# Loads on SyncE's queue in a graph kernel: a window slice from a doubled transpose, the destinations in one DMA, slice addresses made once, row registers loaded 32 at a time

## Chip, cores and metric

One NeuronCore of one Trainium2 chip. The metric is the device time of one execution in microseconds (us), over three runs; smaller is better. Engines go by the profile's names: PE (matmul), PEld (its weight loads), DVE, ACT, POOL (GpSimd) and SP (SyncE). "SPq", "ACTq" and "POOLq" are the queues in which these issue DMAs, load registers and wait.

## The reference

Per edge, a message from its two nodes and its attributes; a sum over the edges that end in a node; a node update with a residual and a layer norm (no scale or shift).

```
x (12500, 64)   src, dst (400000,)   edge_attr (400000, 16)      dst is sorted
m_in     = concat([x[src], x[dst], edge_attr])                   # 400000 x 144
messages = silu(silu(m_in @ W1 + b1) @ W2 + b2)                  # 400000 x 64
agg      = segment_sum(messages, dst, 12500)
h        = x + silu(concat([x, agg]) @ W3 + b3)
out      = (h - mean(h)) / sqrt(var(h) + 1e-5)
```

## The kernel before

**Tiling.** 400000 edges are 3125 tiles of 128 edges. Eight tiles are an oct (1024 edges; 391 octs), three octs a chunk. As dst is sorted, the destinations of an oct lie in a window of S = 48 nodes that begins at `base[o]`, the destination of the oct's first edge; the values of `base` lie in `bi` (one partition, 391 integers). Two tiles share a matmul: the even tile on features 0 to 63, the odd one on 64 to 127.

**The first layer has three parts, summed in PSUM.**

- *Source part*, x[src] times the first 64 rows of W1. In the first 12 octs (RAW) POOL gathers rows of x. Meanwhile a table `pa` of that product for every node is made (L177 to L191), and later octs gather rows of `pa`, 128 rows in an indirect DMA (L382), with no matmul but a transposition (L462). Two of the eight tiles of about half of the octs (196, `pairs`) come another way: ACT copies 72 columns an oct and DVE 64 (L308, L306) out of the resident transposed x at addresses loaded into registers (L299), and a matmul (L465) makes their product. 23 further pairs of tiles (`rpairs`) are fetched by SP row by row: each oct, `rows` loads 16 addresses from `rindex` into registers (L329) and issues 16 DMAs of one 256-byte row of `pa` (L333); 16 octs fill one tile `rx` (256 rows), which the oct after next takes (L462).
- *Destination part*, x[dst] times the next 64 rows of W1, plus b1. SP loads the window's slice of transposed x, 64 features by 48 nodes, twice side by side into `xr` (L401; 3 buffers), whose 65th row is ones. `window_product` (L406) multiplies it with `w1bb` to 96 rows by 128 columns, `window_copy` (L411) multiplies by `mask`, which keeps rows 0 to 47 for the even tile and rows 48 to 95 for the odd one, into rows 0 to 95 of `xw`. `compare_dst` (L433) makes the one-hot matrix `oh`: rows 0 to 47 compare each window node with the even tile's destinations, rows 48 to 95 with the odd one's. The destinations `dr` are loaded for a chunk by two DMAs, 48 equal rows each (L421).
- *Attribute part*: rows 96 to 127 of `xw` are the last 16 rows of W1, those of `oh` the attributes (L422). One matmul of `xw` and `oh` (L466) gives destination and attribute part together.

After silu (L469), the second layer (L478, L480) and its silu (L484), a second one-hot matrix `eh` (L439) sums the messages by window node (L493), and DVE adds the window into `agg` (L498). Node groups of 512 are finished as soon as their edges are (L501 to L568), and what is left after the last oct.

**The order of the work.** The loop at L641 writes the order of PE, ACT, DVE and SP out by hand; each works through its list in order. In iteration o, SP issues: index loads for columns and rows (L360, L344); sometimes a slice of `src` (L123); at a chunk's beginning `dr` and the attributes of the chunk of oct o+3 (L421, L422); the slice `xr` of oct o+3 (L401), before which, every fourth time, four bases are loaded into registers (L390); the 16 rows (L329, L333); and loads and stores of nodes. PE takes in iteration o: the window product of oct o+1, the first layer of oct o, the node products, the sums of oct o-4, the second layer of oct o-2. POOL only gathers, three octs ahead in the order of the program (L669), into five buffers: it stops when the buffer that it needs has not been read by L462. In the built program each DMA of SP waits for the eighth DMA ahead of it on the same queue to have landed.

`window_load` as it is:

```
def window_load(o):
    if o % 4 == 0:
        bases(ENG.SP, o)
    xr = xrs[o % 3]
    frm = xt[:, ds(winreg.pop((ENG.SP, o)), S)]
    nc.sync.dma_start(xr[:D], frm[:, None, :].to_broadcast([D, 2, S]))
    winrow[o] = xr
```

Of the kernel before, what the change touches and what calls it, by code (L numbers as in the profile page):

```python
# [9 lines left out]
F32 = mybir.dt.float32  # L10
BF16 = mybir.dt.bfloat16
I32 = mybir.dt.int32
U8 = mybir.dt.uint8
AF = mybir.ActivationFunctionType
OP = mybir.AluOpType
# [3 lines left out]
ENG = mybir.EngineType  # L19

P = 128
# [3 lines left out]
S = 48  # L25
# [10 lines left out]
ROWS = 16  # L36
# [11 lines left out]
@with_exitstack  # L48
def kernel(
    ctx: ExitStack,  # L50
    tc: tile.TileContext,
    x: bass.AP,
    xt: bass.AP,
    src_c: bass.AP,
    src_row: bass.AP,
    dst_c: bass.AP,
    dst_row: bass.AP,
    attr_t: bass.AP,
    dst_2: bass.AP,
    attr_2: bass.AP,  # L60
    base: bass.AP,
    w1: bass.AP,
    b1: bass.AP,
    w2: bass.AP,
    b2: bass.AP,
    w3: bass.AP,
    b3: bass.AP,
    out: bass.AP,
    edges: int,
):  # L70

    nc = tc.nc
    N, D = x.shape

    const = ctx.enter_context(tc.tile_pool(name="const", bufs=1))
    dram = ctx.enter_context(tc.tile_pool(name="dram", bufs=1, space=DRAM))
    pa = dram.tile([N, D], F32, name="pa")
    badi = const.tile([1, 1], I32, name="badi")
    ident = const.tile([P, P], F32, name="ident")  # L90
    make_identity(nc, ident)

    with ExitStack() as inner:
        windows(inner, tc, ident, badi, pa, x, xt, src_c, src_row, dst_c, dst_row, attr_t, dst_2, attr_2, base, w1, b1, w2, b2, w3, b3, out, edges)

    flag = nc.values_load(badi[0:1, 0:1], min_val=0, max_val=2 * P,
                          skip_runtime_bounds_check_because="a count of partitions")
    with tc.If(flag > 0):
        general(tc, ident, x, xt, src_c, dst_c, dst_row, attr_t, w1, b1, w2, b2, w3, b3, out, edges)


def windows(ctx, tc, ident, badi, pa, x, xt, src_c, src_row, dst_c, dst_row, attr_t, dst_2, attr_2, base, w1, b1, w2, b2, w3, b3, out, edges):
    nc = tc.nc
    N, D = x.shape
    NP = xt.shape[1]
# [4 lines left out]
    E = 2 * S  # L110
    const = ctx.enter_context(tc.tile_pool(name="fconst", bufs=1))

    fast = ctx.enter_context(tc.tile_pool(name="fast", bufs=1))
# [12 lines left out]
    bi = fast.tile([1, NO], I32, name="bi")  # L126
# [69 lines left out]
    bf = fast.tile([1, NO], F32, name="bf")  # L196
# [2 lines left out]
    nc.gpsimd.iota(rowi, pattern=[[1, S]], base=0, channel_multiplier=0)  # L199
    coli = fast.tile([P, 1], I32, name="coli")  # L200
    nc.gpsimd.iota(coli, pattern=[[0, 1]], base=0, channel_multiplier=1)
    colf = fast.tile([P, 2], F32, name="colf")
    nc.vector.tensor_copy(colf[:, 0:1], coli)
    nc.vector.tensor_scalar(colf[:, 1:2], colf[:, 0:1], float(S), None, op0=OP.is_ge)

    mask = fast.tile([P, P], F32, name="mask")
    nc.vector.memset(mask[:, :D], 0.0)
    nc.vector.memset(mask[:, D:], 1.0)
    nc.vector.tensor_scalar(mask, mask, colf[:, 1:2], None, op0=OP.is_equal)
    nc.vector.tensor_scalar(colf[:, 1:2], colf[:, 1:2], -float(S), None, op0=OP.mult)  # L210
    nc.vector.tensor_tensor(colf[:, 0:1], colf[:, 0:1], colf[:, 1:2], op=OP.add)

    wb = fast.tile([P, NO], F32, name="wb")
    wps = ctx.enter_context(tc.tile_pool(name="wps", bufs=1, space=PSUM))
# [3 lines left out]
    pb = mis.tile([P, NO], F32, name="mm")  # L218
    nc.tensor.matmul(pb, ones, bf, start=True, stop=True)
    nc.vector.tensor_copy(wb, pb)  # L220
    nc.vector.tensor_scalar(wn, pb, colf[:, 0:1], None, op0=OP.add)

    rel = dc.bitcast(F32)
# [11 lines left out]
    w1bb = fast.tile([D + 1, 2, D], F32, name="w1bb")  # L235
# [1 line left out]
    nc.sync.dma_start(w1bb[D:, :, :], b1.rearrange("(o s k) -> o s k", o=1, s=1).to_broadcast([1, 2, D]))  # L237
    xrs = []
    for k in range(3):
        t = fast.tile([D + 1, 2, S], F32, name=f"xr{k}")  # L240
        nc.vector.memset(t[D:], 1.0)
        xrs.append(t)
    xw = []
    for k in range(3):
        t = fast.tile([P, P], F32, name=f"xw{k}")
# [10 lines left out]
    with tc.tile_pool(name="gat", bufs=AHEAD + 2) as gat, tc.tile_pool(name="drp", bufs=2) as drp, \  # L256
# [15 lines left out]
        while True:  # L272
            o = RAW + -(-2 * P * (len(pairs) + 1) // RATE) + 2
# [39 lines left out]
        while True:  # L313
            o = RAW + -(-2 * P * (len(rpairs) + 1) // ROWS) + 1
            if o >= len(octs) - 1:
                break
            rpairs.append(o)
        single, rindex = {}, {}
        pab = pa[:, :].bitcast(U8).rearrange("n d -> (n d)")

        def rows(o):
            lo = (o - RAW) * ROWS
            j, e0 = lo // (2 * P), lo % (2 * P)
            if o < RAW or j >= len(rpairs):
                return
            if e0 == 0:
                single[rpairs[j]] = rx.tile([P, 2, D], F32, name="rx")
            t = single[rpairs[j]].bitcast(U8)
            _, regs = nc.values_load_multi_w_load_instructions(  # L329
                rindex[j][0:1, e0:e0 + ROWS], engines=(ENG.SP,), min_val=0, max_val=4 * D * (N - 1),  # L330
                skip_runtime_bounds_check_because="src names a node")
            for e, r in zip(range(e0, e0 + ROWS), regs):
                nc.sync.dma_start(t[e % P:e % P + 1, e // P, :], pab[ds(r, 4 * D)].rearrange("(o n) -> o n", o=1))  # L333

        def rbegun(o):
# [32 lines left out]
                    nc.vector.tensor_scalar(t[:, h], t[:, h], 4.0, float(XBASE[s] + XADDR), op0=OP.mult, op1=OP.add)  # L368

        winrow, winreg = {}, {}  # L370
        sums = psa.tile([P, 4, S], F32, name="pg")

        def gather(o):
# [13 lines left out]
        def bases(eng, o):  # L387

            n = min(4, NO - o)
            _, regs = nc.values_load_multi_w_load_instructions(  # L390
                bi[0:1, o:o + n], engines=(eng,), min_val=0, max_val=N - 1,
                skip_runtime_bounds_check_because="dst names a node")
            for i in range(n):
                winreg[eng, o + i] = regs[i]

        def window_load(o):
            if o % 4 == 0:
                bases(ENG.SP, o)
            xr = xrs[o % 3]
            frm = xt[:, ds(winreg.pop((ENG.SP, o)), S)]  # L400
            nc.sync.dma_start(xr[:D], frm[:, None, :].to_broadcast([D, 2, S]))  # L401
            winrow[o] = xr

        def window_product(o):
            pw = mis.tile([P, P], F32, name="mm")
            nc.tensor.matmul(pw[:E, :], winrow[o].rearrange("k s w -> k (s w)"), w1bb.rearrange("k s m -> k (s m)"),  # L406
                             start=True, stop=True)
            winrow[o] = pw

# [3 lines left out]
        def load(c, o0=0, o1=CT // OT):  # L413

            if c not in loaded:
                loaded[c] = (drp.tile([E, CT // 2 * P], I32, name="dr"), hot.tile([P, CT // 2 * P], F32, name="oh"))
            dr, oh = loaded[c]
            e = slice(o0 * OT // 2 * P, o1 * OT // 2 * P)
            d = slice(c * CT // 2 * P + e.start, c * CT // 2 * P + e.stop)
            for k in range(2):  # L420
                nc.sync.dma_start(dr[k * S:(k + 1) * S, e], dst_2[k:k + 1, d].to_broadcast([S, e.stop - e.start]))  # L421
            nc.sync.dma_start(oh[E:, e], attr_2[:, d])  # L422

        hots = {}
# [159 lines left out]
        for q in range(early):  # L584
            if q >= rest:
                break
            o = lead[due[q]] + LAST - 1
# [4 lines left out]
        for q0, q1 in batches:  # L592
            o = lead[due[q1 - 1]] + LAST - 1
# [28 lines left out]
        for o in range(min(AHEAD, NO)):  # L622
            gather(o)
        window_load(0)
        window_product(0)
        window_copy(0)
        load(0, 0, 1)
        load(0, 1, 3)
        window_load(1)
        window_load(2)  # L630
        relative(0, CT)
        lims = nv.tile([P, 2, LP], F32, name="lims")
# [5 lines left out]
        with tc.manual_schedule(engines={ENG.PE, ENG.Activation, ENG.DVE, ENG.SP}):  # L638
            compare_dst(0)
            compare_nodes(0)  # L640
            for o in range(NO + THIRD):  # L641
# [3 lines left out]
                for k in parts[3 * o - 3:3 * o] if o else []:  # L645
                    n = min(XC, NP - k)
# [23 lines left out]
                if o + 3 < NO and octs[o + 3][3]:  # L670
                    load(octs[o + 3][0])
                if o + 3 < NO:
                    window_load(o + 3)
                if o + 1 < NO:
                    window_product(o + 1)
                if o % 4 == 0 and 4 <= o < NO + 4:
                    bases(ENG.DVE, o - 4)
# [21 lines left out]
                if 30 <= o < 30 + 2 * LP and o % 2 == 0:  # L699
                    k = (o - 30) // 2  # L700
# [10 lines left out]
                address(o + 2)  # L711
                raddress(o + 2)
                rows(o)
                if o < NO:
                    for f, a in todo.get(o, []):
# [284 lines left out]
```

## Time and profile before

| | |
|---|---|
| three runs, median (lowest to highest) | 3422.63 us (3420.27 to 3425.53) |
| the profiled execution, time | 3420.95 us |
| its span in the trace | 3418.8 us |
| granted TensorE clock, mean | 0.697 |
| busy, ACT / POOL / DVE / PE / PEld | 91% / 74% / 71% / 67% / 45% |
| SP row DMAs (L333) | 5888 |
| indirect gathers (L382) | 2591 of `pa`, 96 of x |

The profile is one execution, recorded by the hardware. Its page sums up each engine, each group of instructions by line and the chain of work that ended last; the trace can be asked for waits, for single lines, and for all that ran in a stretch of time. Times of rows count from the span's start. A row of a group reads: line, engine, operation, output<-input, shapes, xcount | busy us, mean ns | idle time before it and what ended that. A row of waits reads: engine, line <- what it waited for: us in total, times, longest us. A row of a line of code reads: durations as minimum/median/maximum in ns. "issue" is time in which the engine waited for nothing that the profile shows.

### The profile page before, as it was taken

How to read it: one execution, taken by the hardware profiler on the slowest of the kernel's cores; microseconds unless marked ns; L12 is line 12 of the kernel's file. 1: busy time of each engine (PE TensorE's matmuls, PEld its weight loads, DVE VectorE, ACT ScalarE, POOL GpSimd, SP SyncE). 2: the span in 40 equal slices, each digit the busy share in tenths (PEclk: the TensorE clock that was granted, in tenths of full speed). 3: DMA queues.
4: the chain of work that ended last, by engine and by line, in shares of the span. 5: the costliest groups of instructions: out<-in, count | busy, mean ns of one | idle time of the engine just before them, and what ended most of it. 6: DMA issues, size and time to landing. Idle time of an engine off the chain costs nothing. (4 is left out here: it accounts for less than half of the span.)

```text
span 3418.8 us, 107012 instructions
## 1 busy us (share of the span) xinstructions
PE 2283.9 (67%) x13764; PEld 1545.4 (45%) x13764; DVE 2433.6 (71%) x26003; ACT 3109.1 (91%) x27413; POOL 2542.7 (74%) x2696
## 2 busy tenths in 40 slices
PE   6777776666666666666666656666667576666667
PEld 4545444444444444444444444434444354444444
DVE  2577777677776777778777777777787776877772
ACT  2499999999999999999999999998999999999992
POOL 7777777777777777777777777776777777777774
PEclk7756566676666777677676667776766766777766
DMA  6532233233333322323332233233223223332322
GB/s 136 119 64 61 62 65 65 62 63 67 69 61 65 66 61 63 68 60 66 72 62 59 62 69 60 62 69 66 62 61 68 61 61 69 65 62 60 69 60 58
DMA packets 202928, 229.05 MB, mean 67 GB/s; under 512 B 133023, under 2 KB 141413, under 8 KB 201301
## 3 DMA queue, kind: packets, MB, share of 16 engines
q1 hardware_dynamic: 101560, 122.63, 16.1%
q0 software_dynamic: 85984, 88.22, 13.8%
q10 hardware_dynamic: 14652, 11.26, 1.5%
q14 instruction: 615, 5.03, 0.5%
q8 instruction: 117, 1.92, 0.2%
HBM read 215.45 MB, written 6.40 MB: 65 GB/s over the span
## 5 line engine op out<-in xcount | busy, mean ns | idle before, releaser
L382 POOL DMA_INDIRECT ga<-pa,sc x2591 | 2449.8, 945 | 813.4 <-issue 702.5
L308 ACT COPY cx<-xs 64x4 uint8 x26568 | 2646.4, 187 | 60.7 <-issue 37.2
L306 DVE TENSOR_REDUCE cx<-xs 64x4 uint8 x23608 | 1684.2, 153 | 527.3 <-issue 477.2
L406 PE MATMUL mm<-w1bb,xr 65*96 65x128 f32 x782 | 234.6, 395 | 839.2 <-DMA xr<-in_xt 673.6
L466 PE MATMUL p<-oh,xw 128*128 128x512 f32 (+1 forms) x758 | 601.7, 890 | 0.0
L480 PE MATMUL p<-w2d,h 128*128 128x128 f32 x3126 | 571.7, 339 | 0.0
L406 PEld LDWEIGHTS mm<-w1bb,xr 65*96 65x96 f32 x782 | 141.0, 226 | 890.3 <-DMA xr<-in_xt 785.1
L493 PEld LDWEIGHTS pg<-eh,m 128*64 128x64 f32 x6250 | 283.0, 175 | 574.6 <-issue 368.2
L480 PEld LDWEIGHTS p<-w2d,h 128*128 128x128 f32 x3126 | 483.1, 236 | 114.7 <-issue 114.7
L493 PE MATMUL pg<-eh,m 128*64 128x48 f32 x6250 | 334.8, 263 | 104.8 <-DVE agg L498 101.8
L433 DVE TENSOR_TENSOR oh<-dr,wrow 96x512 f32<-96x512 int32 x391 | 263.6, 674 | 150.4 <-DMA dr<-in_dst 70.8
L462 PE MATMUL p<-ident,ga 128*128 128x128 f32 x1296 | 318.9, 372 | 68.4 <-DMA ga<-pa,sc 68.1
L469 ACT ACTIVATE h<-p 128x512 f32<-128x512 f32 x391 | 231.7, 592 | 144.8 <-PE p L466 99.9
L462 PEld LDWEIGHTS p<-ident,ga 128*128 128x128 f32 x1296 | 236.1, 196 | 84.6 <-issue 80.3
L484 ACT ACTIVATE m<-p 128x512 f32<-128x512 f32 x391 | 231.4, 592 | 43.5 <-PE p L480 31.2
L439 DVE TENSOR_TENSOR eh<-wrow,dc 128x384 f32<-128x384 f32 x391 | 214.3, 548 | 2.7
L498 DVE TENSOR_TENSOR agg<-agg,pg 128x48 f32 x391 | 78.2, 200 | 188.3 <-PE mm L533 113.3
L466 PEld LDWEIGHTS p<-oh,xw 128*128 128x128 f32 x758 | 179.6, 291 | 0.0
L478 PE MATMUL p<-b2r,one 3*128 3x512 bf16 x391 | 177.5, 454 | 0.0
L411 DVE TENSOR_TENSOR xw<-mm,mask 96x128 f32<-96x128 f32 x391 | 109.6, 280 | 23.1 <-PE mm L406 15.2
L382 POOL DMA_INDIRECT ga<-in_x,sc x96 | 90.8, 946 | 30.2 <-issue 28.0
L465 PE MATMUL p<-cx,w1d 128*128 128x128 f32 x392 | 109.9, 377 | 0.0
(84 smaller groups left out, 780.2 us busy)
## 6 DMA issues: line engine op xcount, KB each, us to landing
rx<-pa SPq DMA_DIRECT2D x5888, 0.2 KB
dr<-in_dst SPq DMA_DIRECT2D x260, 288.0 KB
ga<-pa,sc POOLq DMA_INDIRECT x2591
oh<-in_attr SPq DMA_DIRECT2D x130, 192.0 KB
xr<-in_xt SPq DMA_DIRECT2D x391, 24.0 KB
xs<-in_xt ACTq DMA_DIRECT2D x12, 512.0 KB
cxi<-in_src_row SPq DMA_DIRECT2D x196, 1.0 KB
pa<-v ACTq DMA_DIRECT2D x12, 256.0 KB
```

The lines of the kernel that those rows point to most:

```text
L306: nc.vector.tensor_reduce(to, frm[:, :, None], AX.X, OP.max)
L308: nc.scalar.copy(to, frm)
L382: nc.gpsimd.indirect_dma_start(out=ga[:, i, :], out_offset=None, in_=x if o < RAW else pa[:, :], in_offset=bass.IndirectOffsetOnAxis(ap=sc ...
L406: nc.tensor.matmul(pw[:E, :], winrow[o].rearrange("k s w -> k (s w)"), w1bb.rearrange("k s m -> k (s m)"), start=True, stop=True)
L433: nc.vector.tensor_tensor(oh[:E, :], dr[:, e:e + w], wn[:E, o:o + 1].to_broadcast([E, w]), op=OP.is_equal)
L439: nc.vector.tensor_tensor(eh[:, :n], row[:, None, :].to_broadcast([P, n, S]), rel[:, t0:t0 + n, None].to_broadcast([P, n, S]), op=OP.is_equal)
L462: nc.tensor.matmul(p1[:, i, :], g2.rearrange("p s d -> p (s d)"), ident, is_transpose=True, start=(i == c), stop=False, skip_group_check=True)
L466: nc.tensor.matmul(p1[:, :k], xw[o % 3], oh, start=False, stop=True, skip_group_check=True)
L469: nc.scalar.activation(h[:, :k], p1[:, :k], AF.Silu)
L480: nc.tensor.matmul(p2[:, 2 * i:2 * i + 2, :].rearrange("p s d -> p (s d)"), h[:, i, :], w2d, start=False, stop=(i == k - 1), skip_group_ch ...
L484: nc.scalar.activation(m[:, :n2], p2[:, :n2], AF.Silu)
L493: nc.tensor.matmul(pg[s * D:(s + 1) * D, :], m[:, i, :], eh[:, i, :], start=(i < 2), stop=(i >= n - 2), skip_group_check=True)
```

## The change

Four edits. (1) The host passes a second transposed x, `xt2`, in which each column stands twice in a row (node n in columns 2n and 2n+1), and the slice is one DMA of 64 rows of 2 x 48 neighbouring elements, addressed in bytes. Rows of the window product, of `xw` and of `oh` are thereby ordered node by node, even and odd tile in turn, and the mask and the window node of each row are made from the row number by a shift and an `and`. (2) So the destinations are one DMA of 96 rows, whose source alternates between the two rows of `dst_2`. (3) The bases are multiplied by 8 once by DVE, into the storage of `bf` (free once its matmul has read it), and SP loads the slice's byte address. (4) Row addresses are loaded 32 at a time, in even octs, and used in two octs. The number and order of the other DMAs and of the work of PE, ACT, DVE and POOL in the loop stay.

```diff
+    half = fast.tile([P, 2], I32, name="half")
+    nc.vector.tensor_scalar(half[:, 0:1], coli, 1, None, op0=OP.arith_shift_right)
+    nc.vector.tensor_scalar(half[:, 1:2], coli, 1, None, op0=OP.bitwise_and)
     colf = fast.tile([P, 2], F32, name="colf")
-    nc.vector.tensor_copy(colf[:, 0:1], coli)
-    nc.vector.tensor_scalar(colf[:, 1:2], colf[:, 0:1], float(S), None, op0=OP.is_ge)
+    nc.vector.tensor_copy(colf, half)
...
-    nc.vector.tensor_scalar(colf[:, 1:2], colf[:, 1:2], -float(S), None, op0=OP.mult)
-    nc.vector.tensor_tensor(colf[:, 0:1], colf[:, 0:1], colf[:, 1:2], op=OP.add)
...
+    bi8 = bf.bitcast(I32)
+    nc.vector.tensor_scalar(bi8, bi, 8.0, None, op0=OP.mult)
...
-        t = fast.tile([D + 1, 2, S], F32, name=f"xr{k}")
+        t = fast.tile([D + 1, 2 * S], F32, name=f"xr{k}")
...
-            _, regs = nc.values_load_multi_w_load_instructions(
-                rindex[j][0:1, e0:e0 + ROWS], engines=(ENG.SP,), min_val=0, max_val=4 * D * (N - 1),
-                skip_runtime_bounds_check_because="src names a node")
-            for e, r in zip(range(e0, e0 + ROWS), regs):
+            if o % 2 == 0:
+                _, rowreg[:] = nc.values_load_multi_w_load_instructions(
+                    rindex[j][0:1, e0:e0 + 2 * ROWS], engines=(ENG.SP,), min_val=0, max_val=4 * D * (N - 1),
+                    skip_runtime_bounds_check_because="src names a node")
+            for e in range(e0, e0 + ROWS):
+                r = rowreg.pop(0)
                 nc.sync.dma_start(t[e % P:e % P + 1, e // P, :], pab[ds(r, 4 * D)].rearrange("(o n) -> o n", o=1))
...
+        xt2b = xt2.bitcast(U8)
...
+            at, unit = (bi8, 8) if eng == ENG.SP else (bi, 1)
             _, regs = nc.values_load_multi_w_load_instructions(
-                bi[0:1, o:o + n], engines=(eng,), min_val=0, max_val=N - 1,
+                at[0:1, o:o + n], engines=(eng,), min_val=0, max_val=unit * (N - 1),
...
-            frm = xt[:, ds(winreg.pop((ENG.SP, o)), S)]
-            nc.sync.dma_start(xr[:D], frm[:, None, :].to_broadcast([D, 2, S]))
+            nc.sync.dma_start(xr[:D, :].bitcast(U8), xt2b[:, ds(winreg.pop((ENG.SP, o)), 8 * S)])
...
-            for k in range(2):
-                nc.sync.dma_start(dr[k * S:(k + 1) * S, e], dst_2[k:k + 1, d].to_broadcast([S, e.stop - e.start]))
+            nc.sync.dma_start(dr[:, e], dst_2[None, :, d].to_broadcast([S, 2, e.stop - e.start]))
             nc.sync.dma_start(oh[E:, e], attr_2[:, d])
...
+        "xt2": np.repeat(np.concatenate([x, np.zeros((P, d), x.dtype)]).T, 2, axis=1),
```

More of the change, by code (lines that the diff above doesn't have):

```diff
@@ L53 @@
     xt: bass.AP,
+    xt2: bass.AP,
     src_c: bass.AP,
@@ L93 @@
     with ExitStack() as inner:
-        windows(inner, tc, ident, badi, pa, x, xt, src_c, src_row, dst_c, dst_row, attr_t, dst_2, attr_2, base, w1, b1, w2, b2, w3, b3, out, edges)
+        windows(inner, tc, ident, badi, pa, x, xt, xt2, src_c, src_row, dst_c, dst_row, attr_t, dst_2, attr_2, base, w1, b1, w2, b2, w3, b3, out, edges)
     flag = nc.values_load(badi[0:1, 0:1], min_val=0, max_val=2 * P,
@@ L99, with windows @@
         general(tc, ident, x, xt, src_c, dst_c, dst_row, attr_t, w1, b1, w2, b2, w3, b3, out, edges)
-def windows(ctx, tc, ident, badi, pa, x, xt, src_c, src_row, dst_c, dst_row, attr_t, dst_2, attr_2, base, w1, b1, w2, b2, w3, b3, out, edges):
+def windows(ctx, tc, ident, badi, pa, x, xt, xt2, src_c, src_row, dst_c, dst_row, attr_t, dst_2, attr_2, base, w1, b1, w2, b2, w3, b3, out, edges):
     nc = tc.nc
@@ L317, in windows @@
             rpairs.append(o)
-        single, rindex = {}, {}
+        single, rindex, rowreg = {}, {}, []
         pab = pa[:, :].bitcast(U8).rearrange("n d -> (n d)")
@@ L405, in window_product @@
             pw = mis.tile([P, P], F32, name="mm")
-            nc.tensor.matmul(pw[:E, :], winrow[o].rearrange("k s w -> k (s w)"), w1bb.rearrange("k s m -> k (s m)"),
+            nc.tensor.matmul(pw[:E, :], winrow[o], w1bb.rearrange("k s m -> k (s m)"),
                              start=True, stop=True)
```

## The prediction

> **What bounds the kernel now.** I read the page first, then the waits, then POOL in stretches of 100 us, then the trace around single octs.
>
> ```profile
> span 3418.8 us, 107012 instructions
> PE 2283.9 (67%) x13764; PEld 1545.4 (45%) x13764; DVE 2433.6 (71%) x26003; ACT 3109.1 (91%) x27413; POOL 2542.7 (74%) x2696
> L382 POOL DMA_INDIRECT ga<-pa,sc x2591 | 2449.8, 945 | 813.4 <-issue 702.5
> ```
>
> By busy time ACT is the engine to look at. But 702.5 us of POOL's idle time is "issue": nothing that the profile shows held it. The waits say how it is made up:
>
> ```profile
> POOL ga L382 <- issue: 730.5, 2396, 0.3
> POOL ga L382 <- DMA ga<-pa,sc: 58.0, 190, 0.3
> POOL ga L382 <- PE p L462: 34.9, 38, 3.8
> PEld mm L406 <- DMA xr<-in_xt: 785.1, 209, 9.2
> ```
>
> The longest "issue" is 0.3 us: a pause of 0.3 us follows every gather, so a gather costs 1.25 us and not the 0.945 shown. Only the third row holds real stops (up to 3.8 us): the buffer was not free, because PE was late. And PE's great wait is for the slice `xr`.
>
> ```profile
> 2.76 1.11 POOL L382 DMA_INDIRECT ga<-in_x,sc  x1 [1.27 <-DMA sc<-in_src_c]
> 289.64 0.94 POOL L382 DMA_INDIRECT ga<-pa,sc  x1 [0.30 <-issue]
> 1994.96 0.95 POOL L382 DMA_INDIRECT ga<-pa,sc  x1 [0.30 <-issue]
> 3369.39 1.23 POOL L602 IOTA xs<- 128x393 int32 x1
> 3385.79 1.06 POOL L382 DMA_INDIRECT ga<-pa,sc  x1 [0.30 <-issue]
> 300.00:400.00 100.00, 75.60 (x81) 0.59 0.31 66
> 1800.00:1900.00 100.00, 75.61 (x81) 0.66 0.30 63
> 2300.00:2400.00 100.00, 70.40 (x76) 0.68 0.31 64
> 3000.00:3100.00 100.00, 72.23 (x76) 0.70 0.31 64
> ```
>
> These are gathers number 1, 230 and 1594, POOL's one other operation in the loop, gather 2687, then POOL's busy time in four stretches of 100 us (behind it granted clock, DMA share, GB/s). From 1 to 1594: 1992.2 / 1593 = 1.2506 us each, and the stretches up to 1900 us are full (75.6). At that pace the last would start at 2.76 + 2686 x 1.2506 = 3361.9 us, 3363 with L602 (1.23). It starts at 3385.8: **POOL is the bound, and loses some 23 us in stops, all in the second half**. Behind the last gather come 33 us of tail.
>
> Why there? Gathers 230 and 1594 end octs 30 and 230 (an oct is 6.87 gathers on average, by the code). The slices of the same octs on SP's queue:
>
> ```profile
> 278.77 0.63 SPq L401 DMA_DIRECT2D xr<-in_xt  x1
> 2008.64 0.60 SPq L401 DMA_DIRECT2D xr<-in_xt  x1
> SPq L333 <- DMA oh<-in_attr: 19.1, 47, 1.3
> SPq L401 <- PE p L466: 10.9, 24, 0.7
> SPq L333 <- DMA dr<-in_dst: 6.7, 12, 1.1
> SPq L333 <- DMA xr<-in_xt: 5.3, 14, 1.1
> ```
>
> SP's period is 1729.9 / 200 = 8.65 us an oct, POOL's 1705.3 / 200 = 8.53. SP falls behind by 0.123 us an oct: from 10.9 us ahead of the last gather of its oct to 13.7 us behind it. The four waits are the longest of SP's queue between 300 and 2000 us: 42 us of 1700. SP is not held, it is full. When its lag has eaten POOL's five buffers (the stretches are full to 1900 us), POOL stops too. One such place:
>
> ```profile
> 1016.42 5.11 SPq L333 DMA_DIRECT2D rx<-pa  x16
> 2330.72 0.79 SPq L421 DMA_DIRECT2D dr<-in_dst  x2
> 2331.61 0.69 SPq L422 DMA_DIRECT2D oh<-in_attr  x1
> 2332.48 0.61 SPq L401 DMA_DIRECT2D xr<-in_xt  x1
> 2334.66 5.44 SPq L333 DMA_DIRECT2D rx<-pa  x16
> 2336.21 0.68 DVE L433 TENSOR_TENSOR oh<-dr,wrow 96x512 f32<-96x512 int32 x1 [2.59 <-DMA dr<-in_dst]
> 2337.35 0.74 PE L406 MATMUL mm<-w1bb,xr 65*96 65x128 f32 x2 [5.99 <-DMA xr<-in_xt]
> 2339.21 0.94 POOL L382 DMA_INDIRECT ga<-pa,sc  x1 [3.81 <-PE p L462]
> ```
>
> (The first row is an oct without a wait: 5.11 / 16 = 0.32 us a row DMA.) The slice goes out at 2332.48, PE has it at 2337.35 after waiting 6 us, then L462 frees the buffer, and POOL goes on 3.5 us late.
>
> **The change part by part.** Nothing changes in the loop on POOL, PE, ACT or DVE: every term is SP's time per oct. To keep POOL from stopping, the drift over the 360 octs behind oct 30 must stay under the 24.6 us that the buffers took before: under 0.068 an oct, so SP must save 0.055.
>
> ```profile
> L329 SPq TENSOR_LOAD <-rxi x368: 972/1415/1439, 129.1 to 3327.2; - x184
> L390 SPq TENSOR_LOAD <-bi x98: 302/557/914, 7.7 to 3349.8; - x98
> L401 SPq ALU_OP  x391: 32/41/54, 8.3 to 3358.9; - x196
> L401 SPq DMA_DIRECT2D xr<-in_xt x391: 598/615/1432, 8.5 to 3359.0; - x196
> L421 SPq DMA_DIRECT2D dr<-in_dst x264: 311/408/1577, 9.3 to 3356.3; - x132
> L147 ACTq DMA_DIRECT2D xs<-in_xt x14: 472/558/702, 2.5 to 116.1; - x14
> L515 SPq DMA_DIRECT2D xa<-in_x x25: 331/366/579, 267.9 to 3360.3; - x25
> 5.04 0.57 DVE L220 COPY wb<-mm 128x391 f32<-128x391 f32 x1 [1.01 <-PE mm L219]
> ```
>
> *Register loads.* No load of 32 is in the trace. 4 registers take 302 ns at least, 16 take 972: 56 ns a register. The median of 16 is 1415; I read the 440 ns between as a start cost that is spared in the one oct of four where a base load stands just ahead. A pair of loads is 2 x (0.75 x 1415 + 0.25 x 972) = 2.61 us; one of 32 is 972 + 16 x 56 + 440 = 2.31. Saved 0.30 a pair, 0.15 an oct. Bounds: with the steepest slope of these rows, (1415 - 302) / 12 = 93 ns, it would take 2.90 (0.14 lost an oct); without the 440, 1.87 (0.37 saved). The Trainium skill, "DMA: Bandwidth & Descriptors", section "Latency and other measured facts", gives a register load a floor of about 600 ns; by that each load dropped is worth 0.3 us an oct instead of 0.15. The 302 ns of the row speak for the smaller value.
>
> *Slice address*: 41 ns of ALU an oct, saved. *Slice DMA*: 128 pieces of 192 bytes become 64 of 384. Rows for 64 pieces exist on ACT's queue (558 median, 472 least, 702 most), for 128 on SP's (366). I take 0.50: 0.115 saved; bounds 0.09 lost, 0.25 saved. *Destinations*: two of 408 (0.79 together) become one of 96 rows; nothing shows it. Between one of the old (408) and the two together; I take the old slice's 0.6: 0.2 a chunk, 0.07 an oct; bounds 0 and 0.13.
>
> *What it costs.* SP's DMAs wait for the eighth ahead. Behind `dr`, attributes and slice, the sixth row is the eighth behind `dr`. Before, the register load (1.4) stood between slice and rows; these waits were 19.1 + 6.7 + 5.3 = 31.1 us in 66 chunks, 0.47 each. Chunks begin in turn in even and odd octs. In an odd one no load stands there now: the sixth row is ready 0.6 + 0.4 + 0.5 + 0.3 (gaps) + 5 x 0.32 = 3.4 us behind `dr`, which lands up to 5.5 us behind its issue (2336.21 - 2330.72): a wait of 2.1, with base loads before half of them 1.9. In an even one the load of 2.3 covers it. On average 1.0 a chunk, 0.5 more than now: 0.18 an oct lost. Bounds: all waits go (0.16 saved), or every chunk waits 2.1 (0.54 lost).
>
> Sum: 0.15 + 0.04 + 0.115 + 0.07 - 0.18 = **0.2 us an oct saved; SP's period 8.45**, below POOL's 8.53. With SP no longer behind, PE gets slices early, and POOL runs at 1.25 us to the end. What is late next is POOL itself, on which nothing is changed.
>
> *Start.* The first base load now waits for DVE's multiplication, which stands behind L220 (ends 5.61, so ready about 6.2); SP comes to that load at 7.7. It costs nothing, and a few us there would be covered by POOL's buffers. The operations on row numbers are two fewer or three more of 0.15 us.
>
> *Time.* The profiled execution took 3420.95, 2.15 more than its span; the median of three is 1.7 higher, and stops that vary from run to run are part of that. 3418.8 - 23 + 2.15 = **3398 us**.
>
> **The rivals.** *Part of it*: SP saves between 0 and 0.055; the drift shrinks, POOL stops later and less: 3403 to 3416. For it: four of five terms are not in the trace. Chance 0.12.
>
> *Another engine holds the pace* (no difference). The Trainium skill, "Perfetto Trace Analysis", section "Identifying the Most-Contended Engine", takes the engine with the highest occupancy as the one to relieve; that is ACT, and SP's work would not matter. In rows:
>
> ```profile
> 300.00:2000.00 1700.00, 1129.01 (x6792) 763.52 (x6792) 1266.79 (x13759) 1628.77 (x14565) 1284.76 (x1361) 0.69 0.31 64
> PE mm L406 <- DMA xr<-in_xt: 673.6, 186, 13.9
> ```
>
> The first row has the busy times of PE, PEld, DVE, ACT and POOL in that order. ACT: 1628.8 us in 199 octs, 8.2 an oct, 0.3 below POOL's pace. For it: that is thin, and compute was never seen without SP's delay. Against it: PE waits for slices, not for ACT. If some other chain holds compute at 8.65, or SP's terms cancel: 3416 to 3428. Chance 0.10.
>
> *Slower: the single `dr` lands later than its halves did*, and SP, which works in order, waits for it. SP's other terms save 0.375 an oct, 1.1 a chunk; it turns when the waits of a chunk pass 0.47 + 1.1 = 1.6 us on average (I expect 1.0). Landing 2 us later, odd chunks would wait 3.9 and even ones 1.8: (2.85 - 0.47) / 3 - 0.375 = 0.42 an oct more, all of it POOL's: 360 x 0.42 = 150 us, about 3570. For it: the landing of one DMA of that size is not in the trace. Against it: the same bytes, issued over the same 0.8 us. Chance 0.12.
>
> **How the numbers follow.** Forecast 0.66 (3391 to 3403), part 0.12, none 0.10, slower 0.12. The likeliest is 3398. From 3391 (a shorter tail) to 3418 (all but the upper part of no change) lie about 8 in 10; the worst ends of all terms together (0.7 an oct lost, some 260 us) lie with the slower 0.12. 0.2% is 6.8 us, about what can be told from no change. Faster by more: 0.66 + 0.12 less a little, 0.77. Within: 0.11. Slower: 0.12.
>
> **What would show it.** Right: POOL 75.6 busy in every stretch of 100 us to 3300; waits of POOL for L462 under 15 us; the wait of L406 for `xr` far smaller; SP's L401 ahead of its oct's last gather, and waits of SP for PE in its place; one load of 32 at about 2.3 us, the slice at 0.5, `dr` at 0.6; rows waiting 2 us for `dr` in odd chunks. Wrong: L401 still drifting; long waits of L333 for `dr`; or ACT or DVE waits ahead of PE.

## The result, and the profile after

| | median (lowest to highest) | runs |
|---|---|---|
| before, beside it | 3424.08 us (3420.27 to 3430.72) | 4 |
| after | 3396.59 us (3396.16 to 3401.12) | 4 |

The ratio is 0.9921, 95% interval 0.9903 to 0.9939: faster by 0.6 to 1.0%. The forecast was 3398, its own range 3391 to 3403. The profiled execution of after took 3396.16 us, 1.8 more than its span.

The experiments below ran on several chips, and the kernel before takes 3412 to 3434 us on two of them and 5509 to 5539 on four, so each experiment is set only against runs of before on its own chip.

First the page of after: span, busy times, the gathers, and the packets of all DMAs.

```profile
span 3394.4 us, 106238 instructions
PE 2398.6 (71%) x13764; PEld 1581.2 (47%) x13764; DVE 2430.3 (72%) x26003; ACT 3108.1 (92%) x27413; POOL 2542.1 (75%) x2696
L388 POOL DMA_INDIRECT ga<-pa,sc x2591 | 2449.2, 945 | 790.0 <-issue 707.6
DMA packets 175783, 228.98 MB, mean 67 GB/s; under 512 B 105886, under 2 KB 114276, under 8 KB 174164
```

By these sums hardly anything happened: ACT, DVE and POOL are as busy as before to within 4 us, and PE is busier by 115 us at a slightly lower granted clock (0.684 against 0.697), without effect on the end. The gain shows in POOL's waits and in its stretches of 100 us (length, POOL's busy time, granted clock, DMA share, GB/s).

```profile
POOL ga L388 <- issue: 734.7, 2410, 0.3
POOL ga L388 <- DMA ga<-pa,sc: 54.9, 180, 0.3
POOL ga L388 <- PE p L467: 8.5, 28, 0.3
PEld mm L412 <- DMA xr<-in_xt: 433.9, 166, 7.8
```
```profile
300.00:400.00 100.00, 75.61 (x81) 0.59 0.30 66
1800.00:1900.00 100.00, 75.61 (x81) 0.62 0.30 64
2300.00:2400.00 100.00, 75.60 (x81) 0.74 0.29 65
3000.00:3100.00 100.00, 75.47 (x81) 0.70 0.28 63
```

L467 is the transposition that frees a gather's buffer. Its row fell from 34.9 us with stops of up to 3.8 to 8.5 us with nothing above 0.3, and 0.3 is the ordinary pause behind every gather: POOL never stops for a buffer now. The two late stretches hold 81 and 81 gathers, where before held 76 and 76. PE's wait for the slice is about half of what it was.

The timeline shows the two queues against each other: gathers 230, 1594 and 2687 on POOL, and the slices of octs 30 and 230 on SP.

```profile
278.53 0.52 SPq L407 DMA_DIRECT2D xr<-in_xt  x1
290.66 0.94 POOL L388 DMA_INDIRECT ga<-pa,sc  x1 [0.30 <-issue]
1983.46 0.47 SPq L407 DMA_DIRECT2D xr<-in_xt  x1
1995.56 0.94 POOL L388 DMA_INDIRECT ga<-pa,sc  x1 [0.30 <-issue]
3362.45 1.05 POOL L388 DMA_INDIRECT ga<-pa,sc  x1 [0.30 <-issue]
```

The slice goes out 12.1 us ahead of its oct's last gather at oct 30 and 12.1 ahead at oct 230; before, it went from 10.9 ahead to 13.7 behind. SP's period is (1983.46 - 278.53) / 200 = 8.525 us an oct, and POOL's (1995.56 - 290.66) / 200 is 8.525 too: SP no longer falls behind. The last gather starts at 3362.45 instead of 3385.79, 23.3 us earlier, and the tail behind it is 31.95 instead of 33.0: together the 24.4 us by which the span is shorter.

SP's instructions by line (least, median, most in ns); the last row is that of before, for the row above it:

```profile
L333 SPq TENSOR_LOAD <-rxi x184: 2287/2308/2336, 132.8 to 3271.9; - x184
L407 SPq DMA_DIRECT2D xr<-in_xt x391: 468/495/1306, 8.7 to 3330.4; - x196
L426 SPq DMA_DIRECT2D dr<-in_dst x132: 578/634/1502, 9.2 to 3316.0; - x132
L397 SPq TENSOR_LOAD <-bf x98: 307/556/837, 7.7 to 3301.9; - x98
L427 SPq DMA_DIRECT2D oh<-in_attr x132: 316/542/1596, 9.9 to 3329.9; - x132
L422 SPq DMA_DIRECT2D oh<-in_attr x132: 310/367/811, 10.5 to 3358.5; - x132
```

and SP's longest waits between 300 and 2000 us (us in total, times, longest):

```profile
SPq L338 <- DMA dr<-in_dst: 35.6, 33, 2.7
SPq L365 <- ACTq L302: 21.1, 19, 4.4
SPq L338 <- DMA oh<-in_attr: 18.0, 36, 1.1
...
SPq L338 <- DMA xr<-in_xt: 5.1, 12, 0.9
```

The row DMAs (L338) wait 58.7 us in 66 chunks, where they waited 31.1. A new wait stands beside them: L365 loads an index tile that ACT still reads. Over all rows of this view SP's waits for other engines come to 68 us, where they came to 37 before: SP is held by the others more than it was, and at these octs it is still 12 us ahead, no more and no less. The attributes' DMA, which nothing in the change touches, takes 0.17 us longer behind the new destinations.

### The profile page after: what moved, and what is told of

Its sections match the earlier page's. It is cut to its first block, busy times and chain, and to the rows that moved or that the text cites. A ratio compares the mean times of both kernels' runs of the same rounds, so it can differ in the third digit from the quotient of the medians.

```text
span 3394.4 us, 106238 instructions
## 1 busy us (share of the span) xinstructions
PE 2398.6 (71%) x13764; PEld 1581.2 (47%) x13764; DVE 2430.3 (72%) x26003; ACT 3108.1 (92%) x27413; POOL 2542.1 (75%) x2696
## 2 busy tenths in 40 slices
DMA packets 175783, 228.98 MB, mean 67 GB/s; under 512 B 105886, under 2 KB 114276, under 8 KB 174164
## 5 line engine op out<-in xcount | busy, mean ns | idle before, releaser
L471 PE MATMUL p<-oh,xw 128*128 128x512 f32 (+1 forms) x758 | 623.0, 919 | 0.0
L485 PE MATMUL p<-w2d,h 128*128 128x128 f32 x3126 | 604.5, 353 | 0.0
L498 PEld LDWEIGHTS pg<-eh,m 128*64 128x64 f32 x6250 | 301.0, 184 | 619.9 <-issue 381.9
L485 PEld LDWEIGHTS p<-w2d,h 128*128 128x128 f32 x3126 | 512.0, 248 | 124.2 <-issue 124.2
L467 PE MATMUL p<-ident,ga 128*128 128x128 f32 x1296 | 358.8, 374 | 296.6 <-DMA ga<-pa,sc 295.5
L412 PE MATMUL mm<-w1bb,xr 65*96 65x128 f32 x782 | 226.1, 383 | 471.1 <-DMA xr<-in_xt 357.7
L498 PE MATMUL pg<-eh,m 128*64 128x48 f32 x6250 | 354.1, 273 | 131.7 <-DVE agg L503 118.7
L467 PEld LDWEIGHTS p<-ident,ga 128*128 128x128 f32 x1296 | 232.5, 190 | 366.3 <-issue 340.7
L483 PE MATMUL p<-b2r,one 3*128 3x512 bf16 x391 | 187.3, 479 | 0.0
```

Source lines behind the costliest of these rows:

```text
L412: nc.tensor.matmul(pw[:E, :], winrow[o], w1bb.rearrange("k s m -> k (s m)"), start=True, stop=True)
L467: nc.tensor.matmul(p1[:, i, :], g2.rearrange("p s d -> p (s d)"), ident, is_transpose=True, start=(i == c), stop=False, skip_group_check=True)
L471: nc.tensor.matmul(p1[:, :k], xw[o % 3], oh, start=False, stop=True, skip_group_check=True)
L485: nc.tensor.matmul(p2[:, 2 * i:2 * i + 2, :].rearrange("p s d -> p (s d)"), h[:, i, :], w2d, start=False, stop=(i == k - 1), skip_group_ch ...
L498: nc.tensor.matmul(pg[s * D:(s + 1) * D, :], m[:, i, :], eh[:, i, :], start=(i < 2), stop=(i >= n - 2), skip_group_check=True)
```

## The experiments

The theory was that of the prediction: SP's queue, full, delays the slices, PE frees POOL's buffers late, and the change takes 0.2 us an oct from SP, of which only what POOL lost can come back. Rival A: the fewer packets (202928 to 175783) or shorter transfers bring the gain, not the time of SP's queue. Rival B: only all edits together are enough, or one edit that was not priced as decisive carries it.

### The slice alone

Before, with edits 1 and 3 (slice of 64 rows, addresses made once). The register loads stay as before; the node-by-node order of rows needs every second partition in the two DMAs of `dr`:

```diff
-                nc.sync.dma_start(dr[k * S:(k + 1) * S, e], dst_2[k:k + 1, d].to_broadcast([S, e.stop - e.start]))
+                nc.sync.dma_start(dr[k:E:2, e], dst_2[k:k + 1, d].to_broadcast([S, e.stop - e.start]))
```

> The same kernel as in e2_slice_alone, beside runs of the kernel before on the same chip, since those of e2_slice_alone stood at 5528 us for the kernel before. Where the kernel before takes 3420 to 3431 us again: theory (SP's queue time): 615 - 495 ns of the DMA and 41 ns of ALU saved, 0.16 us an oct, no new wait: SP's period 8.49, under POOL's 8.53; POOL never stops, 3397 us (3394 to 3402). Rival 'the loads are the whole gain': 3422. Rival 'fewer packets': 3397.

Measured: 3396.6 us (3394.98 to 3402.23, 5 runs) against 3420.59 (8 runs), ratio 0.9935, interval 0.9914 to 0.9956. That can't be told from the whole change. SP's lines, then the two queues in the timeline:

```profile
L405 SPq DMA_DIRECT2D xr<-in_xt x391: 468/515/907, 8.4 to 3329.6; - x196
L425 SPq DMA_DIRECT2D dr<-in_dst x264: 511/577/1332, 9.0 to 3317.3; - x132
```
```profile
279.29 0.52 SPq L405 DMA_DIRECT2D xr<-in_xt  x1
289.88 0.94 POOL L386 DMA_INDIRECT ga<-pa,sc  x1 [0.30 <-issue]
1992.51 0.51 SPq L405 DMA_DIRECT2D xr<-in_xt  x1
1994.20 0.94 POOL L386 DMA_INDIRECT ga<-pa,sc  x1 [0.30 <-issue]
3361.76 0.97 POOL L386 DMA_INDIRECT ga<-pa,sc  x1 [0.30 <-issue]
```

SP's period is 1713.22 / 200 = 8.566 us an oct, POOL's 1704.32 / 200 = 8.522. Between these octs SP still falls behind, by 0.044 an oct (10.6 us ahead at oct 30, 1.7 at oct 230), but that is under the 0.068 that the prediction worked out as bearable. Behind oct 230 it falls back no farther: the slice of oct 380 goes out at 3270.79, 8.522 us an oct. PE still waits 685.7 us for slices:

```profile
PEld mm L410 <- DMA xr<-in_xt: 685.7, 186, 8.8
POOL ga L386 <- PE p L466: 10.4, 34, 0.3
```

and POOL doesn't stop once over 0.3 us. So the time is decided by whether the drift eats POOL's five buffers before the end, not by how long PE waits. The period was 0.08 longer than expected (8.49). Each of the two `dr` DMAs takes 577 ns instead of 408 when it writes every second partition, 0.34 a chunk or 0.11 an oct, and the attributes' DMA behind them 536 instead of 367, 0.06 an oct. Against that the rows wait 11 us for landings instead of 31.1, 0.10 an oct less, because the longer issues cover more of them. SP's longest waits between 300 and 2000 us:

```profile
SPq L363 <- ACTq L302: 10.4, 13, 4.5
SPq L405 <- PE p L470: 8.7, 21, 0.6
SPq L336 <- DMA oh<-in_attr: 7.4, 17, 1.3
```

So SP waits for others in this kernel too, and 8.566 is not what its own work needs. Rival A foretold this result as well, because the slice alone also has the fewer packets. Rival B falls with this run: one part of the change is enough.

On another chip, where before takes 5528.22:

> Edits (1) and (3) alone: the slice from the doubled transpose and addresses made once; dr by two DMAs again (each on every second partition), 16 addresses a load. Theory (SP's queue time): 615 - 495 ns of the DMA and 41 ns of ALU saved, 0.16 us an oct, no new wait: SP's period 8.49, under POOL's 8.53; POOL never stops, 3397 us (3394 to 3402). So one edit alone gives the whole gain. Rival 'the loads are the whole gain': 3422. Rival 'fewer packets': 3397 as well, since the packets that went are those of the slice.

Measured: 5520.19, ratio 0.999, interval 0.9979 to 1.0002, no difference that can be told from none. There something else holds the kernel (below), so this answers nothing about 3420.

### The loads of 32 alone

Before, with edit 4 alone (the lines of the change's diff from `if o % 2 == 0` to `rowreg.pop(0)`).

> The same kernel as in e1_load32_alone (edit (4) alone), whose neighbour, the kernel before, stood at 5528 us there. Where the kernel before takes 3420 to 3434 us: theory (SP's queue time): 0.15 us an oct saved by the load, about as much lost by rows that wait for the two halves of dr in odd chunks, where no load stands ahead of them: SP's period 8.6 to 8.65, POOL still stops, 3412 to 3424 us; waits of the row DMAs for dr and attributes between 300 and 2000 us 60 us or more, against 31. Rival 'the loads are the whole gain': 3397.

Measured: 3418.65 us (3409.48 to 3426.98, 10 runs) against 3424.4 (12 runs), ratio 0.9974, interval 0.996 to 0.9989. The load by its line, SP's waits between 300 and 2000 us, POOL's wait for its buffers, and the slices of octs 30 and 230 in the timeline:

```profile
L330 SPq TENSOR_LOAD <-rxi x184: 2039/2312/2333, 130.1 to 3321.2; - x184
```
```profile
SPq L335 <- DMA dr<-in_dst: 38.4, 43, 1.8
SPq L335 <- DMA oh<-in_attr: 15.5, 30, 0.8
...
SPq L335 <- DMA xr<-in_xt: 3.8, 11, 0.8
```
```profile
POOL ga L384 <- PE p L464: 35.3, 42, 3.7
```
```profile
279.75 0.61 SPq L403 DMA_DIRECT2D xr<-in_xt  x1
2018.57 0.66 SPq L403 DMA_DIRECT2D xr<-in_xt  x1
```

The load takes 2.31 us as worked out, and the rows then wait 57.7 us for `dr`, attributes and slice instead of 31.1: 26.6 / 199 octs = 0.13 an oct, nearly all of the 0.15 that the load was worth. Over all rows of that view SP's waits for other engines grow too, from 37 to 47 us. SP's period, 1738.82 / 200 = 8.694, is no shorter than before, and POOL stops as it did. The load that was taken away had covered the landing of `dr`. The median is 5.7 us lower all the same; these rows don't show where from, and its interval reaches to 0.1%.

> The kernel before with edit (4) alone: 32 row addresses in one load. Theory (SP's queue time): a load of 2.31 us instead of two of 2.61 together saves 0.15 us an oct, but in odd octs nothing stands any longer between the slice and the rows, so that the rows of every second chunk wait for the two halves of dr, about 0.16 an oct. Net about 0: SP's period stays at 8.6 to 8.65, POOL still stops, 3412 to 3424 us. Rival 'the loads are the whole gain': 3397. Rival 'fewer packets in the transfers': they are as before, 3422.

Measured on the slower chip: 5522.7 against 5528.22, ratio 0.9989, interval 0.998 to 0.9999. As good as nothing there too.

### All but one edit

After without edit 2 (the two DMAs of the diff above), and after without edit 4 (a load of 16 in each oct). These were to show whether the gain stays with any one edit gone.

> The change without edit (2): dr by two DMAs, each on every second partition. Theory (SP's queue time): slice 0.16 and loads 0.15 saved, 0.16 lost by rows that wait for dr in odd chunks, 8.50 an oct: POOL hardly stops, 3396 to 3403 us. Waits of the row DMAs for dr and attributes of about 1 us a chunk, as in the changed kernel. Rival 'the single dr DMA is needed': 3410 or more.

> The change without edit (4): 16 addresses a load, each oct. Theory (SP's queue time): slice 0.16 and dr 0.05 to 0.07 saved, and no loss of cover: waits of the rows for dr go back to 0.5 us a chunk or less. SP's period 8.43 or lower, if it is not held by others: 3397 us, POOL without stops, SP as far ahead as in the changed kernel or farther. Rival 'the loads are the whole gain': 3415 to 3424.

> The same kernel as in e4_all_but_load32 (the change without edit (4)), whose neighbour, the kernel before, stood at 5528 us there. Where the kernel before takes 3420 to 3434 us: theory (SP's queue time): slice 0.16 and dr 0.05 us an oct saved, no loss of cover: waits of the row DMAs for dr and attributes between 300 and 2000 us about 31 us, against 54 in the changed kernel; SP's period 8.44 or held by others at POOL's 8.53, POOL without stops, 3396 us, as the changed kernel within 3 us. Rival 'the loads are needed': 3405 or more.

Measured: 5503.6 against 5528.22 without edit 2, ratio 0.9954 (0.9939 to 0.9969); without edit 4, 5496.01 against 5528.22, ratio 0.9938 (0.9922 to 0.9955), and on yet another chip 5499.47 against 5523.58, ratio 0.9958 (0.9941 to 0.9974). All three fell on chips where before takes 5.5 ms, and the whole change was not timed on these. There three of the four edits are worth 24 to 32 us, and the slice with its addresses 8 that can't be told from none. At 3420 us these two kernels were never timed; that the slice alone brings all of it there makes them less pressing, but doesn't replace them.

### More work for SP, in both kernels

The test of the theory itself. Into after, and likewise into before, go four DMAs of 32 bytes an oct, into a tile that nobody reads, so that SP's queue is full in both:

```diff
+        dose = fast.tile([1, 8, 8], I32, name="dose")
...
+            for k in range(4):
+                nc.sync.dma_start(dose[:, o % 2 * 4 + k], src_row[:, 0:8])
```

> The same kernel as in f5_after_more_sp, whose neighbour, the kernel before, stood at 5518 us there. Where the kernel before takes 3420 to 3431 us: theory (SP's queue time sets compute's pace): SP's own period of about 8.4 becomes 9.6 to 9.7, above POOL's 8.53; compute follows it, POOL stops nearly every oct, and the span is about 3750 us. Rival 'transfers': no change, 3397.

> The kernel before with four more DMAs of 32 bytes an oct on SP's queue, as in f6_before_more_sp, whose neighbour stood at 5518 us. Where the kernel before takes 3420 to 3434 us: theory (SP's queue time): SP full in both, so that the difference to g5_after_more_sp (span 3761) shows the whole saving of the change: 0.2 to 0.3 us an oct, 75 to 105 us, a span of 3835 to 3865. Rival 'the change saves only what it showed, 26 us': 3787. Rival 'transfers': 3422.

Measured, one run each: after with more 3762.98 us (before on that chip 3433.78), before with more 3837.14 (3425.98). The slices of octs 30 and 380 in the timeline and POOL's wait for its buffers, first of after with more, then of before with more:

```profile
287.37 0.52 SPq L410 DMA_DIRECT2D xr<-in_xt  x1
3654.36 0.51 SPq L410 DMA_DIRECT2D xr<-in_xt  x1
```
```profile
POOL ga L391 <- PE p L470: 398.2, 130, 8.1
```
```profile
290.27 0.61 SPq L404 DMA_DIRECT2D xr<-in_xt  x1
3730.04 0.61 SPq L404 DMA_DIRECT2D xr<-in_xt  x1
```
```profile
POOL ga L385 <- PE p L465: 478.1, 139, 8.1
```

The periods over 350 octs are 9.620 and 9.828 us. The difference, **0.208 us an oct**, is what the change saves SP, free of POOL; the prediction said 0.2, and 0.2 to 0.3 was expected for this pair. It is worth 74 us (3837.14 - 3762.98) where SP holds the pace, and 27 where POOL takes over. POOL waits for its buffers 130 and 139 times in some 370 octs, and not in nearly every oct, as was expected of after. Before without the extra DMAs has a period of 8.661 over the same octs (its slice of oct 380 goes out at 3310.03), so that they add 9.828 - 8.661 = 1.17 an oct. An estimate of what SP needs in after without them, if they add as much there, is 9.620 - 1.17 = 8.45 (8.45 predicted).

Rival A falls as far as packets and bytes go: 1472 tiny DMAs make after 366 us longer, while its packets (178740) stay far below before's 202928. A slice that lands sooner doesn't explain the gain either. Where PE waits for a slice, it goes on at the earliest 2.12 us behind the start of the slice's DMA in before and 1.97 in after; 0.15 us sooner is a shift by one amount, and can't undo a lag that grows by 0.123 an oct. That the slice's DMA holds the queue for less time because it has half as many pieces is no rival, but a part of the theory.

> The changed kernel with four more DMAs of 32 bytes an oct on SP's queue, behind the rows, into a tile that nobody reads: 4 x 0.32 = 1.28 us an oct of SP's time, hardly a byte more. Theory (SP's queue time sets compute's pace): SP's own period of about 8.4 becomes 9.6 to 9.7, above POOL's 8.53; compute follows it, POOL stops nearly every oct, and the span is about 188 (slice of oct 20) + 360 x 9.6 + 110 = 3750 us. Rival 'transfers': 6000 packets of 176000 more, no change, 3397.

> The kernel before with the same four DMAs an oct. Theory (SP's queue time): SP's period 8.65 + 1.28 = 9.9, or 9.8 if some of its waits are covered: 188 + 360 x 9.8 + 110 = 3830 us, up to 3870. With SP full in both, the difference to f5_after_more_sp shows the whole saving of the change, also what POOL hid: 0.2 to 0.3 us an oct, 75 to 105 us. Rival 'transfers': 3422, and the difference stays 26.

The same pair on a chip where before takes 5518.01: 5529.65 and 5596.56, 67 us apart. Only the pair is comparable; how much of the 5.5 ms SP's queue decides there isn't settled by it.

### A version meant to beat both

After with less work for POOL and more for DVE (and a little for SP): 202 instead of 196 pairs of tiles come by column copies, which leaves 2675 of 2687 gathers.

```diff
-VCOLS = (16, 16, 16, 16)
+VCOLS = (17, 17, 17, 17)
...
-LOADS = (16, 16)
+LOADS = (20, 20)
```

> The changed kernel with VCOLS of 17 instead of 16 (DVE copies 68 columns an oct instead of 64) and up to 20 registers a load for columns: 202 pairs instead of 196, so 12 gathers less on POOL (2675). Theory (POOL is the bound in the changed kernel and paced by 1.25 us a gather): 12 x 1.25 = 15 us less, span 3379, 3382 us against 3397, if DVE (6.4 us busy and 1.3 us of issue an oct, of 8.53) carries 4 more columns, about 0.5 us an oct. Rival 'ACT or DVE is the bound, as its share of busy time says': the same or slower, 3397 to 3430, with stops of POOL for buffers.

Measured: 6388.84 us against 5512.85, ratio 1.1584, interval 1.1568 to 1.16. It fell on a chip of the 5.5 ms kind. The waits of DVE's and POOL's largest groups in this kernel and DVE's loads of copy addresses into registers, then the same of after without edit 4 on another such chip:

```profile
DVE cx L309 <- issue: 3472.3, 1644, 4.7
POOL ga L388 <- PE p L467: 2942.2, 355, 17.2
L302 DVEq TENSOR_LOAD <-cxi x1663: 305/3821/4094, 222.9 to 6296.3; - x185
```
```profile
DVE cx L309 <- issue: 1817.5, 2805, 6.1
POOL ga L386 <- PE p L465: 1906.4, 274, 16.0
L302 DVEq TENSOR_LOAD <-cxi x1568: 592/1098/1291, 220.7 to 5388.4; - x196
```

DVE's idle time by "issue" ahead of the column copies went from 1817.5 to 3472.3 us, and POOL's stops from 1906 to 2942. What the expectation left out are the loads: with up to 17 addresses a load on DVE the median is 3.82 us, with up to 16 it is 1.10, and all of DVE's loads together take 4.6 ms instead of 1.6. So it is no better version there. Loads of 16 take the same 1.10 us where before takes 3420 us; if those of this kernel are as long there too, which wasn't tried, they alone outlast the 3397 us of after. Why they are so long is open, and so is whether relieving POOL by another way is worth anything.

## Why the prediction was right, by its steps

**The bound.** Right. POOL's last gather was put at 3363 and starts at 3362.45; the stops of 23 us in the second half are gone, and nothing else moved the time by more than the tail's 1 us. Two readings carried this: the gather's start to start instead of its busy time, and SP's period against POOL's. The Trainium skill, "Perfetto Trace Analysis", section "GPSIMD Engine Instruction", advises just that, to time GpSimd's instructions by the spacing of their starts; here the spacing is 1.25 us where the row shows 945 ns. The rule of the same page that was weighed as a rival, to relieve the engine with the highest occupancy, would have left the time at that of before: ACT is at 92%, as it was (91%), and the time fell by 0.8%.

Two statements on the bound went too far. "SP is not held, it is full" was put too strongly: the four waits shown are 42 us, but all of SP's waits in that stretch are 68, and 37 of them, 0.19 an oct, are for other engines, more than the lag of 0.123. That SP's own work decides is shown by the pair with more work, not by those rows. The wait of PE for slices was to become far smaller and is still 434 us (785 before), 686 with the slice alone: slices needn't come early, only in time for POOL's five buffers.

**The terms of the sum.** The load of 32 was put at 2.31 us and takes 2.308, the slice at 0.50 and takes 0.495, the destinations at 0.6 and take 0.634. The price from slope and start cost held: 972 + 16 x 56 + 440 = 2308. For the slice and the destinations the prediction only chose a value between wide bounds (0.37 to 0.70 and 0.41 to 0.79); that both came within 0.04 is partly luck. A floor of about 600 ns to a register load, which the Trainium skill ("DMA: Bandwidth & Descriptors", "Latency and other measured facts") gives, appears nowhere in these rows: loads of four take 307 at least and 556 in the median.

**The wait that was added.** Right in kind and a little too dear. The rows' waits were put at 1.0 us a chunk and are 58.7 / 66 = 0.89, which makes (0.89 - 0.47) / 3 = 0.14 an oct instead of 0.18. They fall where the prediction had them: between octs 30 and 230 the chunks that begin in odd octs wait 1.6 us on average (1.9 predicted), the others 0.16 (none predicted). With the durations as they came, the sum is 0.15 + 0.04 + 0.12 + 0.05 - 0.14 = 0.22, beside the 0.208 measured with SP full. Two terms that it leaves out nearly cancel, which is luck: the attributes' DMA takes 542 ns instead of 367, 0.06 an oct lost, and with the ALU instruction a pause of 0.05 ahead of it went. The rival with a late `dr` needed 3.9 in odd chunks and more than 1.6 on average over all; with 1.6 and 0.89 it is out.

**SP's period.** Forecast 8.45; in after it reads 1704.93 / 200 = 8.525, which is POOL's period. This is no failure of the sum: SP no longer sets the pace and is held by the others. But the prediction had SP wait for PE then, and its waits for PE stay at 24 us between 300 and 2000 us (25 before); it is ACT (21 against 4) and DVE (23 against 9) that it waits for longer. What SP needs is seen only where it is made the bound again, and there the estimate is 8.45.

**What the prediction didn't say**, though its threshold held it: that 0.055 of the 0.2 would do. The slice with its addresses is enough by itself; the other two edits buy slack. Nor did it say that the loads of 32 are, alone, worth next to nothing, because their gain and the wait that they uncover are of one size (0.15 and 0.13). Whether edits 2 and 4 without the slice would also pass the threshold wasn't tried.

## What to carry to other kernels

Compare the period of each in-order queue with that of the bound over hundreds of turns: a queue that was slower by 1.4% showed no long wait of its own, ran the buffers dry in the second half, and then set the time. A saving on such a queue pays only until the next bound; to measure what it is worth in itself, load that queue equally in both versions. And before an instruction is taken off a queue, ask which landing it was covering.

## What the runs showed of the hardware

- The same kernel took 3412 to 3434 us on two chips and 5509 to 5539 on four. What differs is not the length of the instructions of ACT, DVE and POOL: ACT's column copies have a median of 188 ns in both, DVE's of 148 and 149, and the gathers a mean of 945 and 946. In the loads of 32 alone on a chip of the second kind, against 37.2 us in the profile of before:

```profile
ACT cx L308 <- issue: 1735.7, 2310, 6.5
POOL ga L384 <- PE p L464: 1873.4, 254, 16.1
```

  ACT idles for 1736 us without a wait that the profile names, DVE likewise (1787 us, against 477), and POOL stops behind them. The granted clock is lower there too (0.584 against 0.697), and PE's matmuls are longer (L466, 890 ns: 985 there). But one run of the slice alone there shows a granted clock of 1.0 and took 5536.96 us, the longest of its ten. The cause isn't known.
- A DMA of 48 rows issued in 408 ns onto neighbouring partitions and in 577 onto every second one; one of 96 rows from two alternating sources took 634. The attributes' DMA issued behind them took 367 behind the first, 536 behind the second and 542 behind the third.
- Four DMAs of 32 bytes an oct made SP's period 1.17 us longer, 0.29 each.
- DVE's loads of up to 17 addresses into registers took 3.82 us in the median, those of up to 16 took 1.10; why is not known.
